# The in-place scaling of raw weights on GpSimd: a scalar per partition in place of a product with a spread tensor

## The chip, the cores and the metric

The kernel runs on one core of a Trainium2 chip. The metric is the device time in microseconds (us) of one execution of the whole program. Five engines work side by side and meet through semaphores: TensorE (PE in the profile, with its weight loads as PEld), VectorE (DVE), ScalarE (ACT), GpSimd (POOL) and SyncE (SP), which here issues the DMAs. Each engine takes its own instructions strictly in the order in which the program holds them.

## The reference

One pre-norm decoder layer on x, 8 sequences of 128 tokens by 512 features, in three parts, each added to x:

```python
x = x + _L0_attn_ref(_layernorm(x), w_q, w_k, w_v, w_o)      # 32 heads, 8 KV heads, head size 128, causal
x = x + _L0_xattn_ref(ctx, ctx, _layernorm(x))               # one head per sequence, 128 x 128 scores over 512 features
x = x + _L0_ffn_ref(_layernorm(x), gate..., up..., down...)  # 4-bit packed weights, inner size 1376
```

Self-attention, the part around the change, is

```python
q = (h @ w_q).reshape(B, S, 8, 4, 128); k = (h @ w_k).reshape(B, S, 8, 128); v = (h @ w_v).reshape(B, S, 8, 128)
probs = softmax(where(causal, q k^T / sqrt(128), -inf))
out = (probs v).reshape(B, S, 4096) @ w_o
```

w_q is 512 x 4096, w_k and w_v are 512 x 1024, w_o is 4096 x 512, all float32.

## The kernel before

Matrix products are made in pairs of float16: each operand is split in a high part and the rest that the high part leaves out, and a product is the sum of three matmuls (`mm3`, lines 162 to 164: high by high, high by low, low by high). A weight must therefore go through three steps before PE can use it: it is multiplied by a scale that brings it into the range of float16, the high part is a cast to float16, and the low part is the difference.

The work goes by KV heads (`g` = 0 to 7), each in two halves of four sequences, 64 attention steps in all. A step works on one head group and one sequence (`g`, `b`): `att_s` makes the scores of the next step, the softmax (`softmax_rows`, line 558: DVE takes the maxima at L611, ACT the exponentials at L568, DVE the reciprocals at L576, POOL multiplies them by a constant at L578) and the probabilities, which POOL normalises (`s`, L625), ACT casts (`pb`, L116), POOL subtracts (`pb`, L119) and a transposing DMA on SP's queue (L639) turns into `pt`. `att_v` multiplies by v, and its result is split into `ah` (ACT) and `al` (DVE). `att_o` multiplies by w_o and DVE adds into x at L665.

Beside these steps the weights of the next head groups are made ready. `fetch_wq`, `fetch_wk`, `fetch_wv` and `fetch_wo` load raw float32 weights into `rawq`, `rawk`, `rawv` and `rawo` (`rawq`, `rawv`, `rawo` have one buffer each, `rawk` two, so a load must wait until its buffer has been read for the last time). `sumsq` (ACT, L260) sums squares, `scales` (a small matmul and three DVE instructions, the last one the reciprocal at L312) makes a scale per matrix or per head, equal on all partitions, in `scq`, `sck`, `scv`, `sco`. Then `prep_wq`, `prep_wk`, `prep_wv` and `prep_wo` call `convert` on pieces of 128 x 512: the function that the change touches. For the first pieces (`direct`) ACT and DVE do it from the raw weight in two instructions. For all others POOL first scales the raw weight in place (L356), ACT casts (`split`, L116) and POOL subtracts (L119). There are 71 such pieces: 30 of `rawo`, 28 of `rawq`, 7 of `rawk`, 6 of `rawv`. The function `at` hangs these calls on attention steps (lines 1130 to 1150), and `pace["mul"]` keeps a scaling behind the normalisation (L625) of the step that it hangs on.

The order on each engine is not the order of the text. The kernel is built with `schedule_with_timeline_sim=True` (line 1480): a planner takes instructions whose inputs are ready on its own clock, which runs on its own costs, by their place in the text, and the order that comes out is fixed in the program. Orders written out by hand are laid over this: `issue_after` for single instructions, `in_order` for the beginning and, on PE and POOL, for the last attention steps. In the middle, the place of the scalings between the other POOL instructions is the planner's.

After the attention steps come the cross-attention (woven into the last ones) and the feed-forward part (`Chain`, lines 1184 to 1197), in which no raw weight is scaled on POOL. Its weights are unpacked by DVE during the attention steps (`dequant`, L810 and L814), from the loads at L794 and L802 on SP's queue.

Of the kernel before, what the change touches and what calls it, by code (L numbers as in the profile page):

```python
# [14 lines left out]
ALU = mybir.AluOpType  # L15
# [38 lines left out]
def tile_decoder(  # L54
# [19 lines left out]
    nc = tc.nc  # L74
# [40 lines left out]
    def split(hi, lo, src, lo_eng=None):  # L115
        a = nc.scalar.copy(hi, src)  # L116
        if hi.dtype == F32R:
            hi = hi.bitcast(F32)
        b = (lo_eng or nc.vector).tensor_tensor(lo, src, hi, ALU.subtract)  # L119
        return a, b  # L120

    def issue_after(later, earlier):


        tc.add_manual_dep(
            later.ins,
            earlier.ins.name,
            mybir.DependencyInfo(mybir.DependencyClass.NoSync, mybir.DependencyReason.DATA),
            reason="pace",
        )  # L130
# [217 lines left out]
    def convert(hi, lo, raw, sc, direct=False):  # L348
        if direct:
            a = nc.scalar.activation(hi, raw, AF.Copy, scale=sc)  # L350
            b = nc.vector.scalar_tensor_tensor(lo, raw, sc, hi, ALU.mult, ALU.subtract)
            return a, b
        wide = sc
        while len(wide.shape) < len(raw.shape):
            wide = wide.unsqueeze(2)
        a = nc.gpsimd.tensor_tensor(  # L356
            raw, raw, wide.to_broadcast(list(raw.shape)), ALU.mult
        )
        if pace:
            issue_after(a, pace["mul"])  # L360
        b, c = split(hi, lo, raw, nc.gpsimd)
        return a, b, c

    def prep_wq(g, j, direct=False):
        hi = wqp.tile([P, KT, P], F16, name="wqh", tag="wqh")
        lo = wqp.tile([P, KT, P], F16, name="wql", tag="wql")
        wq_t[g * GH + j] = hi, lo
        raw = raw_t["q", g][:, :, j * P : (j + 1) * P]
        return convert(hi, lo, raw, sc_t["q", g][:, j : j + 1], direct)

    def prep_wk(g, direct=False):
        hi = wkp.tile([P, KT, P], F16, name="wkh", tag="wkh")
        lo = wkp.tile([P, KT, P], F16, name="wkl", tag="wkl")
        wk_t[g] = hi, lo
        return convert(hi, lo, raw_t["k", g], sc_t["k", g], direct)

    def prep_wv(pr, i, direct=False):
        hi = wvp.tile([P, 2, 2 * P], F16, name="wvh", tag=f"wvh{i}")
        lo = wvp.tile([P, 2, 2 * P], F16, name="wvl", tag=f"wvl{i}")
        wv_t[pr, i] = hi, lo  # L380
        raw = raw_t["v", pr][:, 2 * i : 2 * i + 2, :]
        return convert(hi, lo, raw, sc_t["v", pr], direct)
# [1102 lines left out]
```

## Time and profile before

| | |
|---|---|
| time, median of 3 runs | 661.36 us (659.74 to 665.2) |
| span of the profiled execution | 659.3 us, 0.4 under the lowest and 2.1 under the median of the runs |
| mean granted TensorE clock | 0.995 |
| PE busy | 630.6 us (96%) |
| DVE, ACT busy | 469.9 us (71%), 440.4 us (67%) |
| POOL busy | 395.8 us (60%), 586 instructions |
| of it the scalings at L356 | 31.4 (`rawo`) + 29.2 (`rawq`) + 7.3 (`rawk`) + 6.2 (`rawv`) = 74.1 us, 71 instructions |
| first and last scaling | 48.4 us and 429.6 us from the start |

The profile is of one execution. No other time is told of that execution than its span, from its first to its last instruction; the runs' times are beside it. Busy time is what an engine worked; a group's row gives its line, engine, operation, tiles, shapes and count, then busy time and mean duration, then the idle time of the engine just before these instructions and what ended it. Matmuls overlap each other: a product of 512 columns is listed with some 378 ns, while the next starts 216 ns after it, so the idle time of PE is a safer reading than its busy time.

### The profile page before, as it was taken

The page shows a single profiled execution, that of the slowest core. Times are in us where ns is not written, and L with a number is a line of the kernel's source. Part 1 is how long each engine was busy: PE and PEld are TensorE (multiplying, and loading weights), DVE is VectorE, ACT ScalarE, POOL GpSimd, SP SyncE. Part 2 cuts the span into 40 slices and gives each one's busy share as a digit, 9 for nine tenths or more (in the row PEclk, how much of TensorE's full clock was granted, in tenths as well). Part 3 has the DMA queues.
Part 4 walks back from the last instruction along what each step waited for, and adds up shares of the span by engine and source line. Part 5 has one row for each costly group of instructions (what it writes and reads, how often), then busy time and mean ns, then how long its engine had stood idle before and what let it go on. Part 6 is the DMA issues. An engine that isn't in the chain of part 4 may idle for free.

```text
span 659.3 us, 12426 instructions
## 1 busy us (share of the span) xinstructions
PE 630.6 (96%) x3992; PEld 341.9 (52%) x3992; DVE 469.9 (71%) x1474; ACT 440.4 (67%) x1238; POOL 395.8 (60%) x586
## 2 busy tenths in 40 slices
PE   8789999899999999999999999899998988999996
PEld 5455545455655555565555565456554444445443
DVE  6845786656767776675778565677776768988986
ACT  5676677465758574666677565976566578867674
POOL 7757497664747795556588597663576247622521
PEclk9999999999999999999999999999999999999998
DMA  9277244945553755455547514242544243112002
GB/s 316 54 174 146 84 46 133 229 105 158 121 157 80 192 130 153 109 152 140 144 112 163 149 37 120 46 103 57 90 76 70 41 86 55 22 27 65 1 1 64
DMA packets 117773, 69.34 MB, mean 105 GB/s; under 512 B 84190, under 2 KB 100593, under 8 KB 117708
## 3 DMA queue, kind: packets, MB, share of 16 engines
q1 hardware_dynamic: 117708, 68.55, 43.7%
q8 instruction: 31, 0.51, 0.3%
q14 instruction: 34, 0.28, 0.1%
HBM read 42.12 MB, written 2.20 MB: 67 GB/s over the span
## 4 chain that ended last, share of the span: by engine, by line
PE 56%; POOL 13%; DMA 10%; DVE 8%; issue 7%; ACT 5%; SPq 1%; DVEq 0%; POOLq 0%; ACTq 0%
PE ps_c L1184 6%; PE ps_c L1185 6%; PE ps_o L164 5%; PE ps_o L162 5%; PE ps_o L163 5%; PE ps_q L163 5%; PE ps_q L162 5%; PE ps_q L164 5%; DMA pt<-pb 3%; DMA rawq<-in_L_attn_w_q_dram 3%; POOL pb L119 3%; DMA rawo<-in_L_attn_w_o_dram 2%; POOL s L625 2%; POOL wql L119 1%; POOL rawo L356 1%
## 5 line engine op out<-in xcount | busy, mean ns | idle before, releaser
L568 ACT ACTIVATE s<-s,negm 128x64 f32<-128x64 f32 (+1 forms) x256 | 93.1, 365 | 31.6 <-DVE negm L611 31.3
L162 PE MATMUL ps_o<-woh,ah 128*128 128x512 f16 x256 | 97.1, 379 | 3.2 <-ACT ah L116 3.2
L162 PE MATMUL ps_q<-hT,wqh 128*128 128x512 f16 (+1 forms) x260 | 98.2, 378 | 1.7 <-DVE ql L119 1.7
L163 PE MATMUL ps_q<-hT,wqh 128*128 128x512 f16 (+1 forms) x260 | 98.2, 378 | 0.0
L164 PE MATMUL ps_q<-hT,wql 128*128 128x512 f16 (+1 forms) x260 | 98.0, 377 | 0.0
L164 PE MATMUL ps_o<-woh,al 128*128 128x512 f16 x256 | 96.9, 379 | 0.6 <-DVE al L119 0.6
L163 PE MATMUL ps_o<-wol,ah 128*128 128x512 f16 x256 | 97.0, 379 | 0.0
L119 POOL TENSOR_TENSOR pb<-s,pb 128x256 f16<-128x256 f32 (+1 forms) x128 | 71.7, 575 | 14.8 <-ACT pb L116 12.4
L665 DVE SCALAR_TENSOR_TENSOR xr<-ps_o,unsc,xr 128x512 f32<-128x512 f32 x64 | 47.8, 747 | 42.5 <-PE ps_o L164 41.9
L611 DVE CUSTOM_DVE_ANT_0 s<-ps_sc,mask,soft 128x64 f32<-128x64 f32 (+1 forms) x256 | 66.9, 309 | 4.3 <-PE ps_sc L164 2.0
L578 POOL TENSOR_SCALAR rec<-rec 128x4 f32<-128x4 f32 x64 | 14.8, 231 | 90.1 <-DVE rec L576 87.4
L625 POOL TENSOR_TENSOR s<-s,rec 128x128 f32<-128x128 f32 (+1 forms) x128 | 64.3, 523 | 4.5
L116 ACT CAST pb<-s 128x256 f16<-128x256 f32 (+1 forms) x128 | 43.0, 350 | 33.7 <-POOL s L625 30.0
L119 DVE TENSOR_TENSOR ql<-ps_q,qh 128x512 f16<-128x512 f32 x64 | 43.9, 686 | 28.8 <-ACT qh L116 28.6
L116 ACT CAST ah<-ps_at 128x512 f16<-128x512 f32 x64 | 37.1, 581 | 23.3 <-PE ps_at L164 10.1
L119 DVE TENSOR_TENSOR al<-ps_at,ah 128x512 f16<-128x512 f32 x64 | 43.7, 683 | 7.0 <-ACT ah L116 6.6
L568 ACT ACTIVATION_READ_ACCUMULATOR s<-s,negm 128x1 f32 x256 | 48.1, 188 | 0.0
L116 ACT CAST qh<-ps_q 128x512 f16<-128x512 f32 x64 | 36.7, 573 | 14.0 <-PE ps_q L164 12.5
L1197 DVE TENSOR_SCALAR ps_c<-ps_c,rTg 128x512 f32<-128x512 f32 (+1 forms) x56 | 40.7, 750 | 7.1 <-PE ps_c L1185 6.8
L356 POOL TENSOR_TENSOR rawo<-rawo,sco 128x512 f32<-128x512 f32 x30 | 31.4, 1053 | 22.5 <-DVE sco L312 20.3
L1195 ACT ACTIVATE ps_c<-ps_c,rTu 128x512 f32<-128x512 f32 (+1 forms) x57 | 36.3, 659 | 11.3 <-PE ps_c L1185 9.2
L164 PE MATMUL ps_sc<-k,ql 128*128 128x64 f16 (+1 forms) x256 | 42.7, 206 | 0.5 <-DVE ql L119 0.5
(243 smaller groups left out, 1728.9 us busy)
## 6 DMA issues: line engine op xcount, KB each, us to landing
rawq<-in_L_attn_w_q_dram SPq DMA_DIRECT2D x8, 1024.0 KB
rawo<-in_L_attn_w_o_dram SPq DMA_DIRECT2D x8, 1024.0 KB, 6.0
zi<-zd SPq DMA_DIRECT2D x26, 256.0 KB, 4.1
vd<-v SPq DMA_DIRECT2D x64, 64.0 KB, 2.6
qr<-_L_ffn_down_qweight_dram SPq DMA_DIRECT2D x10, 256.0 KB
xr<-in_x_dram SPq DMA_DIRECT2D x8, 256.0 KB, 7.7
rawk<-in_L_attn_w_k_dram SPq DMA_DIRECT2D x8, 256.0 KB, 4.5
rawv<-in_L_attn_w_v_dram SPq DMA_DIRECT2D x4, 512.0 KB
```

Source lines behind the costliest of these rows:

```text
L116: a = nc.scalar.copy(hi, src)
L119: b = (lo_eng or nc.vector).tensor_tensor(lo, src, hi, ALU.subtract)
L162: nc.tensor.matmul(ps, lh, rh, start=start and i == 0, stop=False)
L163: nc.tensor.matmul(ps, lh, rl, start=False, stop=False)
L164: nc.tensor.matmul(ps, ll, rh, start=False, stop=stop and i == n - 1)
L568: exp = nc.scalar.activation(v, v, AF.Exp, bias=negm[:, j : j + 1], scale=-1.0, accum_out=sums[:, j : j + 1],)
L611: nc.vector.tensor_tensor_reduce(view, flat(ps, cols[j]), masks[j // 2], soft_t[g][:, j % 2 : j % 2 + 1], BIG, ALU.add, ALU.min, negm,)
L625: mul = nc.gpsimd.tensor_tensor(v, v, rec[:, 2 * k : 2 * k + 2].unsqueeze(2).to_broadcast([P, 2, (k + 1) * HQ]), ALU.mult,)
L665: return nc.vector.scalar_tensor_tensor(xr[b], ps, unsc_t[g], xr[b], ALU.mult, ALU.add)
L1184: nc.tensor.matmul(ps, lh, rh, start=r == 0, stop=False, skip_group_check=r > 0)
L1185: nc.tensor.matmul(ps, lh, rl, start=False, stop=True, skip_group_check=r > 0)
L1197: nc.vector.tensor_scalar(ps, ps, sc, None, ALU.mult)
```

## The change

The scaling of a raw weight stays on POOL, in place, with the same 71 calls and the same order in the text. Before, it was a product of two tensors: the second one is the scale's one column, read again for each element of the row (`to_broadcast`). After, it is `tensor_scalar` with the scale's column as the scalar of each partition, and one tensor input.

```diff
-        wide = sc
-        while len(wide.shape) < len(raw.shape):
-            wide = wide.unsqueeze(2)
-        a = nc.gpsimd.tensor_tensor(
-            raw, raw, wide.to_broadcast(list(raw.shape)), ALU.mult
-        )
+        a = nc.gpsimd.tensor_scalar(raw, raw, sc, None, ALU.mult)
         if pace:
             issue_after(a, pace["mul"])
         b, c = split(hi, lo, raw, nc.gpsimd)
```

## The prediction

> **What bounds the kernel now.** I read the page's table of engines first, then the rows by slice.
>
> ```profile
> PE 630.6 (96%) x3992; PEld 341.9 (52%) x3992; DVE 469.9 (71%) x1474; ACT 440.4 (67%) x1238; POOL 395.8 (60%) x586
> ...
> PE 8789999899999999999999999899998988999996
> ...
> POOL 7757497664747795556588597663576247622521
> ```
>
> PE is busy almost throughout, POOL in six tenths. A faster POOL can therefore pay only where PE stands idle for something that comes through POOL. To see where, I cut the span where the scalings begin and end (48.4 and 429.6 us) and at PE's stalls. The columns are the stretch, its length, then the busy time of PE, PEld, DVE, ACT and POOL, then clock and DMA.
>
> ```profile
> 48.00:80.00 32.00, 32.00 (x188) 17.36 (x186) 20.13 (x71) 21.34 (x57) 19.35 (x23) 0.95 0.54 131
> 80.00:130.00 50.00, 47.33 (x316) 25.36 (x315) 35.15 (x130) 33.45 (x109) 37.96 (x57) 1.00 0.55 123
> 130.00:226.00 96.00, 96.00 (x649) 54.60 (x648) 63.53 (x209) 61.38 (x200) 62.06 (x94) 1.00 0.52 131
> ...
> 270.00:366.00 96.00, 95.49 (x643) 53.02 (x642) 68.16 (x225) 63.29 (x206) 64.85 (x96) 1.00 0.54 134
> ...
> 380.00:404.00 24.00, 23.94 (x171) 14.15 (x169) 14.07 (x53) 15.20 (x48) 23.41 (x32) 1.00 0.18 39
> 404.00:432.00 28.00, 25.08 (x166) 12.92 (x165) 18.13 (x73) 21.86 (x69) 18.45 (x28) 1.00 0.35 96
> ```
>
> From 130 to 226 us PE has no idle time, though POOL spends 62 of 96 us there: what is saved on POOL in such a stretch is worth nothing. PE's idle time is 2.67 us in 80:130, 2.92 in 404:432, and 0.06 + 0.51 + 0.07 + 0.06 in the four stretches between (226:270, 270:366, 366:380, 380:404). That is **6.3 us in all where scalings run**, and nearly the ceiling of the direct gain. One stretch is different: in 380:404 POOL itself is full, 23.41 of 24 us. The list of waits says what PE idles for:
>
> ```profile
> PE ps_at L648 <- DMA pt<-pb: 4.2, 6, 1.7
> ...
> PE ps_o L162 <- ACT ah L116: 3.2, 3, 2.6
> ```
>
> Both come through POOL: `pt` is the transposed `pb`, which POOL finishes at L119. The 2.6 us wait for `ah` is at 413 us, and the chain of waits explains it (start, length, what; all in us):
>
> ```profile
> 400.84 1.00 POOL rawo L356
> 401.84 0.71 POOL rawq L356
> 402.55 0.25 issue
> 402.80 1.05 POOL pb L119 x2
> 403.85 1.12 POOL wol L119
> 404.97 0.12 SPq L639
> ...
> 405.18 6.66 DMA rawo<-in_L_attn_w_o_dram
> 411.84 0.02 issue
> 411.86 0.05 ACT junk L260
> ```
>
> The single `rawo` buffer comes free when POOL has made the last `wol` of the head before, at 404.97. Only then is the next load issued. ACT has the sum of squares of that load at the head of its queue and stands still (2.64 us) until 411.86; the exponentials, and then `ah`, are queued behind it, and PE waits for `ah`.
>
> **The change, step by step.** It removes 71 products and adds 71 operations of another kind, on the same engine and the same data. No DMA, wait or tile is added. The rows that price it:
>
> ```profile
> L356 POOL TENSOR_TENSOR rawo<-rawo,sco 128x512 f32<-128x512 f32 x30 | 31.4, 1053 | 22.5 <-DVE sco L312 20.3 <-ACT junk L260 2.1
> L1002 POOL TENSOR_SCALAR h<-xr,rs,rstd 128x512 f32<-128x512 f32 x16 | 12.3, 767 | 1.2
> L421 POOL TENSOR_SCALAR h<-xr,rs,rstd 128x512 f32<-128x512 f32 x8 | 6.4, 796 | 0.8
> L1229 POOL CAST it<-pr 128x512 f16<-128x512 f32 x7 | 4.3, 610 | 31.4 <-DVE pr L1217 31.3
> ```
>
> The old form's median is 1.039 us. No row shows `tensor_scalar` with one operation and a column as scalar at this size. The nearest is L1002: same engine, shape and type, two columns as scalars, two operations, 0.767 us. Below it lies the cast, with no scalar, at 0.61; above it the slowest two-tensor form of the size that runs in these stretches, `wol` at L119 with 1.179. I take 0.767, as the kind of instruction is the same and a missing second operation should not cost time. So one scaling saves 1.039 - 0.767 = 0.27 us (bounds: a gain of 0.43, a loss of 0.14), and POOL's busy time falls by 71 x 0.27 = **19 us**, from 395.8 to about 376.5 (bounds 30 less, 10 more).
>
> On the path to the end, stall by stall, in the old order:
>
> - 413 us (2.60 us). From 380.5 us to the last `wol`, POOL works through 9 scalings with hardly a pause. All move the release of `rawo` forward: 9 x 0.27 = 2.4 us at most. What may become late instead is the reciprocal (DVE, L576) that POOL's L578 needs: it ended at 389.86 and 397.57, while POOL came to it at 392.22 and 398.58, so 2.4 and 1.0 us of slack. By the second, 7 scalings have saved 1.9; of these 1.0 is safe, the rest only as far as the exponentials move up too, and they partly do, because ACT's casts of `pb` before them wait for POOL (1.69 and 3.03 us). Between 1.0 and 2.4 I take **1.8**.
> - 122 us (1.75 us, for `pt`). The chain runs back over the `zi` load (issued at 113.69, behind a transposing DMA that waited for POOL on SP's queue) to two scalings at 108.68 and 109.68: **0.54**.
> - 88 us (0.93 us, for `pt`). One scaling on the chain, at 80.03, then a `wol` and `pb`: **0.27**.
> - 272 us (0.51 us, for `pt`). One scaling at 267.52 between `s` and `pb`: **0.27**. ACT's second cast of `pb` ends some 1.4 us after the start of `s` (at 399.88 and 401.29 in a step of the same form), and a short scaling would end at 0.96 + 0.75 = 1.7, so the cast doesn't become the next wait.
>
> Sum: 1.8 + 0.54 + 0.27 + 0.27 = 2.9 us. All else of the 19 us lies beside a full PE. After 430 us nothing is scaled; the later parts start earlier and keep their length. The span becomes 659.3 - 2.9 = 656.4, and with the 2.1 us by which the median of the runs lies above the span, **658.5**.
>
> [...]
>
> **The planner is the unknown.** The order on POOL is its own: at 394.45 and 395.44 two scalings stand between `s` and `pb` of one step, though in the text they follow `pb`. If the planner charges the new form otherwise than the old one, it may order POOL, ACT, PE and SP otherwise in all of 48 to 430 us. Nothing in the trace shows its costs. This can gain or lose; the rivals price it.
>
> **The rivals.**
>
> 1. *Hidden anyway* (about 661.4). The saved time goes into idle time in front of L578 (POOL waited 73.6 us for L576 between 48 and 435 us). For it: most of POOL's stretches. Against it: 380:404, where POOL is full.
> 2. *Not what it says* (661 to 663). The form takes as long as the old one, or up to 1.18. At 0.14 more each, the same chains (13 scalings) lose 1.8 us.
> 3. *All stalls go* (653 to 655). Shorter scalings, or an order that uses them, remove all 6.3 us: 655.1; and a quarter of PE's 5.9 us of idle time in 480:550 besides: 653.6. Against it: the `zi` load takes 4.4 us and the transposes 2.8 to 6.0 whatever POOL does.
> 4. *Slower by a new order* (about 670). The mechanism is the one seen at 405 to 415: a sum of squares on ACT, or a scaling on POOL, placed ahead of a softmax while its input is not there yet. POOL stood idle 20.3 us in 4 places for `sco` and 15.7 in 5 for `scq`, so the planner's clock runs ahead of the chip already; of these, only one led to a stall of PE of over 2 us. A new order that turns three more of these nine waits into stalls like that at 413 us (2.60 idle and 0.16 in the pipeline, 2.8 each) costs 8.3: 669.7. It decides once a wait is longer than the lead that the softmax has over PE, and the steps at 88, 122 and 272 show that this lead is at times nothing.
>
> **How the numbers follow.** One per cent is 6.6 us, about what a measurement of this kernel can tell from no change. Forecast (656 to 661) 0.48, hidden 0.12, not what it says 0.05, all stalls gone 0.14, slower by order 0.21. Of the last, 0.02 stays under 668 (one or two new stalls, 664 to 667); of "all stalls gone", 0.01 stays above 654.7. So faster by over 1% 0.13, within 1% 0.68, slower 0.19. The range reaches from 653, under the case in which all stalls go, to 670, where three new stalls end; about 0.15 is left out, most of it above.
>
> **What would show it.** L356 as TENSOR_SCALAR x71 at 0.75 to 0.80 us, 54 us in all; POOL near 376 us. PE's wait for `ah` near 413 us under 1.6 us, with ACT's wait for `rawo` as much shorter; the waits for `pt` near 88, 122 and 272 shorter by 0.3 to 0.5. PE still full in 130:226. Wrong would be: other neighbours of the scalings on POOL, or new waits of PE for `ah` or `pt` where there were none, which is rival 4; a mean near 1.04, which is rival 2; POOL down by 19 us and PE's idle time as before, which is rival 1.

## The result, and the profile after

The changed kernel takes **670.54 us** (median; 669.02 to 675.36) where the kernel before, run beside it, takes 660.82: a ratio of **1.0152** with an interval of 1.011 to 1.0195. It is slower by 1.5%; the forecast was 658.5.

The page of the changed kernel, its table of engines and two rows by slice (line numbers behind line 353 are five lower than before: L356 is now L353, L568 L563, L639 L634):

```profile
span 667.4 us, 12412 instructions
...
PE 634.4 (95%) x3992; PEld 342.4 (51%) x3992; DVE 473.7 (71%) x1474; ACT 436.6 (65%) x1238; POOL 433.6 (65%) x586
...
PE   8799999999999989999998989999998988999996
...
POOL 7759698764849789558596989582567247622521
```

POOL did not lose 19 us of work but gained 37.8 (395.8 to 433.6). The groups on POOL by form (busy time, mean ns of one, then the engine's idle time before them) say why:

```profile
L353 POOL TENSOR_SCALAR rawo<-rawo,sco 128x512 f32<-128x512 f32 x30 | 47.4, 1589 | 15.1 <-DVE sco L312 12.5 <-ACT junk L260 2.2 <-DVE scx L312 0.4
L353 POOL TENSOR_SCALAR rawq<-rawq,scq 128x512 f32<-128x512 f32 x28 | 44.1, 1580 | 16.2 <-DVE scq L312 12.7 <-DVE sck L312 3.5
L997 POOL TENSOR_SCALAR h<-xr,rs,rstd 128x512 f32<-128x512 f32 x16 | 12.3, 767 | 1.2
```

The new form takes 1.58 us where the product of two tensors took 1.04, and twice what the other `tensor_scalar` on the same shape takes in the same trace (L997, 0.767). Seventy-one of them take 112.0 us instead of 74.1.

PE's stalls, cut as in the prediction (the stretch, its length, then the busy time of PE, PEld, DVE, ACT and POOL, then clock and DMA):

```profile
80.00:130.00 50.00, 47.80 (x299) 24.87 (x298) 37.16 (x130) 32.05 (x101) 42.74 (x54) 1.00 0.47 106
130.00:226.00 96.00, 96.00 (x655) 54.79 (x654) 64.05 (x210) 60.05 (x200) 66.89 (x89) 1.00 0.50 128
226.00:270.00 44.00, 40.87 (x264) 21.82 (x263) 30.70 (x106) 30.60 (x105) 37.28 (x49) 0.96 0.75 174
270.00:366.00 96.00, 94.84 (x627) 52.61 (x625) 62.06 (x206) 57.04 (x186) 63.98 (x85) 1.00 0.50 130
366.00:380.00 14.00, 12.39 (x93) 6.45 (x91) 11.59 (x35) 7.99 (x27) 14.00 (x19) 1.00 0.29 61
380.00:404.00 24.00, 21.74 (x141) 12.79 (x140) 12.34 (x47) 15.41 (x48) 20.50 (x25) 1.00 0.56 117
404.00:432.00 28.00, 28.00 (x179) 14.31 (x177) 17.11 (x66) 19.44 (x64) 19.87 (x31) 1.00 0.28 74
```

PE is still full from 130 to 226 us. The stall at 413 us is gone (28.00 of 28), but 226:270 now loses 3.13 us where it lost 0.06, 366:380 1.61 (0.07) and 380:404 2.26 (0.06). From 80 to 432 us that is 10.4 us of idle PE against 6.3. The last scaling starts at 436.7 us instead of 429.6: 7.1 of the 8.1 us by which the span grew are lost by then. Idle time is only a part of them: in 226:270 the clock was 0.96 as well, and 0.04 of 44 us is another 1.8 us by estimate. PE's waits name the links:

```profile
PE ps_o L162 <- ACT ah L116: 5.6, 5, 2.6
...
PE ps_at L643 <- DMA pt<-pb: 2.3, 5, 1.0
PE ps_o L164 <- DVE al L119: 1.8, 4, 0.8
```

The wait for `pt` has fallen from 4.2 to 2.3 us and the wait for `ah` has risen from 3.2 to 5.6. So the stalls are not simply the old ones made longer. The chain of waits at the longest of them (start, length, what):

```profile
227.37 0.10 POOL pb L119
227.47 6.79 DMA rawo<-in_L_attn_w_o_dram
234.28 1.15 ACT junk L260 x2
235.44 0.48 ACT ah L116
```

ACT waited 3.83 us at the head of its queue for a load of `rawo` still on its way, then made the sum of squares, and only then the `ah` that PE stood still for. It is the mechanism that the prediction read at 405 to 415 us of the kernel before, in a place where it was not before. And the order did change: going by operation and tile names in the two traces, 171 of POOL's 586 places and 549 of the 1230 on ACT that name a tile now hold another instruction. Two things have changed at once, then: the price of a scaling, and the order on the engines.

### The profile page after: what moved, and what is told of

Same layout as the page of the kernel before. It is cut to its first block, busy times and chain, and to the rows that moved or that the text cites. A ratio compares the mean times of both kernels' runs of the same rounds, so it can differ in the third digit from the quotient of the medians.

```text
span 667.4 us, 12412 instructions
## 1 busy us (share of the span) xinstructions
PE 634.4 (95%) x3992; PEld 342.4 (51%) x3992; DVE 473.7 (71%) x1474; ACT 436.6 (65%) x1238; POOL 433.6 (65%) x586
## 4 chain that ended last, share of the span: by engine, by line
PE 59%; DVE 11%; POOL 9%; ACT 9%; DMA 8%; issue 4%; SPq 0%; DVEq 0%; ACTq 0%; POOLq 0%
PE ps_c L1179 6%; PE ps_c L1180 6%; PE ps_o L164 5%; PE ps_o L162 5%; PE ps_o L163 5%; PE ps_q L162 5%; PE ps_q L164 5%; PE ps_q L163 5%; DMA rawq<-in_L_attn_w_q_dram 3%; ACT s L563 2%; POOL rawq L353 2%; POOL pb L119 2%; PE ps_v L162 2%; PE ps_v L164 2%; PE ps_v L163 2%
## 5 line engine op out<-in xcount | busy, mean ns | idle before, releaser
L563 ACT ACTIVATE s<-s,negm 128x64 f32<-128x64 f32 (+1 forms) x256 | 93.0, 364 | 47.3 <-DVE negm L606 47.0
L353 POOL TENSOR_SCALAR rawo<-rawo,sco 128x512 f32<-128x512 f32 x30 | 47.4, 1589 | 15.1 <-DVE sco L312 12.5
L353 POOL TENSOR_SCALAR rawq<-rawq,scq 128x512 f32<-128x512 f32 x28 | 44.1, 1580 | 16.2 <-DVE scq L312 12.7
L563 ACT ACTIVATION_READ_ACCUMULATOR s<-s,negm 128x1 f32 x256 | 48.0, 188 | 0.0
```

The source lines that it names most:

```text
L353: a = nc.gpsimd.tensor_scalar(raw, raw, sc, None, ALU.mult)
L563: exp = nc.scalar.activation(v, v, AF.Exp, bias=negm[:, j : j + 1], scale=-1.0, accum_out=sums[:, j : j + 1],)
```

## The experiments

### What the form itself costs

Thirteen forms, six times each, alone on POOL, chained so that they run one after the other (eight of them here; the comments give the lines of the profile):

```diff
+    many(lambda: g.tensor_tensor(a, a, spread, ALU.mult))               # L88
+    many(lambda: g.tensor_scalar(a, a, one, None, ALU.mult))            # L89, the new form
+    many(lambda: g.tensor_scalar(a, a, one, 1.0, ALU.mult, ALU.mult))   # L90
+    many(lambda: g.tensor_scalar(a, a, 1.0, None, ALU.mult))            # L91
     ...
+    many(lambda: g.tensor_scalar(a, a, one, one, ALU.mult, ALU.mult))   # L93
+    many(lambda: g.tensor_scalar(a, a, nil, None, ALU.add))             # L94
     ...
+    many(lambda: g.tensor_scalar(half, half, one, None, ALU.mult))      # L97, 256 columns
     ...
+    many(lambda: g.tensor_scalar(half, half, one, 1.0, ALU.mult, ALU.mult))  # L99
```

> Nothing of the decoder is computed: POOL alone runs 13 forms on float32 tiles of 128 partitions, six times each, one after the other; x is copied to the output. The profile after shows the new scaling with a mean of 1.58 us, where 0.767 was taken from the form with two operations. Theory A: the form with a single operation is what is slow; then all forms with one operation at 512 columns (column or constant, multiply or add, in place or not) take 1.55 to 1.60 and those with two 0.75 to 0.80. Theory B: what is slow is a multiplication as the first operation (the fast row subtracts first); then multiply and multiply take 1.5 to 1.6 too, and a single addition 0.75 to 0.80. Theory C: writing in place; then the form with another destination takes 0.75 to 0.80. The product of two tensors takes 1.04 in each. If the cost is per element, 256 columns take about 0.8 and 1024 about 3.1 in the slow form.

The groups on POOL by form in this kernel (busy time, mean ns of one):

```profile
L89 POOL TENSOR_SCALAR big<-big,one 128x512 f32<-128x512 f32 x6 | 9.4, 1563 | 0.6
...
L94 POOL TENSOR_SCALAR big<-big,nil 128x512 f32<-128x512 f32 x6 | 9.4, 1562 | 0.6
L91 POOL TENSOR_SCALAR big<-big 128x512 f32<-128x512 f32 x6 | 8.9, 1488 | 0.5
L88 POOL TENSOR_TENSOR big<-big,one 128x512 f32<-128x512 f32 x6 | 6.2, 1038 | 3.5 <-DMA big<-in_x_dram 3.1
L97 POOL TENSOR_SCALAR big<-big,one 128x256 f32<-128x256 f32 x6 | 5.5, 922 | 0.6
L93 POOL TENSOR_SCALAR big<-big,one 128x512 f32<-128x512 f32 x6 | 4.6, 767 | 0.6
...
L90 POOL TENSOR_SCALAR big<-big,one 128x512 f32<-128x512 f32 x6 | 4.2, 692 | 0.6
...
L99 POOL TENSOR_SCALAR big<-big,one 128x256 f32<-128x256 f32 x6 | 2.9, 478 | 0.6
```

On 512 columns every form with **one** operation takes 1.49 to 1.56 us, whether it multiplies or adds, by a column or by a constant, in place or (1.563) to another tile, flat or (1.562) on a strided view. Every form with **two** takes 0.69 to 0.77. A second operation that multiplies by 1.0 makes the instruction 2.26 times as fast. From 256 to 512 columns one operation adds 641 ns (2.5 ns per column), two add 214 (0.84); some 0.28 and 0.26 us do not depend on the size. So the slow part is paid per element. Theory A of the expectation holds, B and C do not. What inside POOL makes it so, no run here shows.

### Price and order apart

With `planned` and `pin` a kernel is built with one form in the order that the planner made for another. The order is planned once, kept by place in the text, and each instruction is chained to the one before it on its engine, without a wait (shortened):

```diff
+    order = planned(new_nc, "tensor_tensor")   # or "one": each engine's order, by place in the text
     ...
         tile_decoder(tc, *args)
+        for places in order.values():
+            for a, b in zip(places, places[1:]):
+                tc.add_manual_dep(made[b], made[a].name, NoSync)
```

The new form in the old order, and the old form in the new one:

> The new operation, with every engine held to the order that the planner made for the kernel before (each engine's instructions are chained). Theory P (price): the operation is 0.55 us longer at 71 places, and the old order has little room for it where POOL is full; 9 of them lie ahead of the load of rawo at 405 us alone, so 5 us there, and half to one us each at 88, 122 and 272 us: 668 to 674 us, at least as slow as the kernel after. Theory O (order): the longer operation hides in idle time of POOL and the loss of the kernel after is its new order: 661 to 664 us.

> The old product of two tensors, with every engine held to the order that the planner made for the kernel after. Theory P: at the old price the new order is about as good as the old one: 659 to 663 us. Theory O: the order carries the loss: 668 to 671 us.

The chaining itself was controlled with the old form in its own order:

> A control: the old product, every engine held to its own old order by the same chaining as in the other runs. If chaining does nothing but fix the order, the time is that of the kernel before, 659 to 662 us; anything else is a cost of the chaining and has to be taken off the runs in the old order.

| time in us, ratio to before [95%] | old order | order of the changed kernel |
|---|---|---|
| product of two tensors, 1.04 us | 661.3, 1.001 [0.9992, 1.0028] | 667.4, 1.0105 [1.0064, 1.0145] |
| one operation, 1.58 us | 679.2, 1.0279 [1.0251, 1.0307] | 670.5, 1.0152 [1.011, 1.0195] |

In the traces of all four kernels each engine's operations and tiles stand in the order that the table says. The chaining, controlled in the old order, costs nothing that can be measured. In the old order the price alone costs some 18 us, more than either theory had put it (668 to 674 at most). The new order alone costs 6 to 7 us at the old price, between the two theories. Together they cost less than the price alone: **the planner's new order gives back about 8.7 us of what the form costs**, and is itself worse than the old order as long as a scaling is cheap.

PE's waits with the new form in the old order show the price at work (waited for, us in all, times, longest):

```profile
PE ps_at L648 <- DMA pt<-pb: 15.8, 16, 4.5
PE ps_o L162 <- ACT ah L116: 5.0, 6, 1.8
```

Four windows of the same kernel, with the columns as above:

```profile
80.00:130.00 50.00, 44.15 (x270) 22.53 (x269) 30.28 (x116) 30.69 (x99) 42.64 (x54) 0.97 0.50 108
...
122.00:126.00 4.00, 0.20 (x2) 0.18 (x2) 2.54 (x4) 1.09 (x3) 4.00 (x6) 1.00 1.06 174
126.00:130.00 4.00, 4.00 (x14) 1.56 (x13) 0.75 (x2) 0.71 (x2) 1.71 (x2) 0.58 0.72 133
404.00:432.00 28.00, 23.61 (x151) 12.52 (x150) 12.48 (x48) 15.66 (x50) 22.28 (x30) 1.00 0.33 84
```

PE now waits sixteen times for `pt`, 15.8 us in all, where it waited six times for 4.2: `pt` comes through POOL, and in the old order scalings stand between `s` and `pb`. The stall at 122 us grows to 4.5 us while POOL works through (4.00 of 4), and behind it the clock falls to 0.58 for the last window before 130 us. So these are stalls of the old kind, for `pt`, longer and more of them.

The old form in the new order has other stalls. Its list of PE's waits:

```profile
PE ps_o L162 <- ACT ah L116: 5.5, 3, 2.8
...
PE ps_o L164 <- DVE al L119: 2.5, 4, 1.6
PE ps_at L648 <- DMA pt<-pb: 1.8, 3, 1.0
```

And two of its windows:

```profile
226.00:270.00 44.00, 40.62 (x271) 22.06 (x270) 30.26 (x97) 29.44 (x99) 36.34 (x52) 1.00 0.77 169
...
380.00:404.00 24.00, 21.05 (x131) 12.11 (x129) 12.47 (x38) 13.38 (x38) 17.97 (x23) 0.93 0.36 88
```

They stand where those of the changed kernel stand, and are about as large (3.38 and 2.95 us against 3.13 and 2.26), though each scaling takes 0.54 us less. So the waits for `ah` at these two places come with the order, the many waits for `pt` in the old order with the price.

### The fast forms of the same instruction

If the single operation is the whole fault of the form, a second operation that changes nothing should give what the prediction wanted. Built with the planner's own order, and held to the old order and to that of the changed kernel (what the edits here and below come to; in the runs the form is chosen in a helper):

```diff
-        a = nc.gpsimd.tensor_scalar(raw, raw, sc, None, ALU.mult)
+        a = nc.gpsimd.tensor_scalar(raw, raw, sc, 1.0, ALU.mult, ALU.mult)
```

> A scalar per partition as in the kernel after, but with a second operation, a multiplication by 1.0; the planner makes its own order. Theory A: each scaling takes 0.75 to 0.80 us, POOL's busy time is near 376 us, and the forecast's sum can be seen at last: 656 to 661 us, or up to 666 where the new order costs something. Theory B: each takes 1.5 to 1.6 and the time is that of the kernel after, 668 to 672 us.

> The scaling with two operations (0.692 us in the run that measured the forms, 0.347 less than the old product) in the old order, so that nothing but the price changes. The forecast's own sum with this price: 0.347 x 9 ahead of the load of rawo at 405 us, capped by the wait of 2.6 us there, take 2.2; 0.69 at 122, 0.35 at 88, 0.35 at 272 us; 3.6 in all, 657 us. The rival (hidden anyway): POOL's saved time goes into waits for other engines, 660 to 661 us.

> The short scaling with two operations in the order that the planner made for the kernel after. With the old product this order took 667 us, 7 more than the old order. If that loss hangs on the places of the sums of squares and loads in the order (ACT waiting for a load at 231 and 385 us) and not on POOL's speed, the time stays at 664 to 667 us; if POOL's speed sets it, it falls by the same 3 us as in the old order or more, to 660 to 664.

And once with the multiplication as the second operation, behind an addition of zero, in the old order:

```diff
+        a = nc.gpsimd.tensor_scalar(raw, raw, 0.0, sc, ALU.add, ALU.mult)
```

> The scaling as the addition of 0.0 and a multiplication by the scale, the two-operation form that the forecast took its price from (0.767 us), in the old order. The forecast's sum as it stands: 2.9 us less than before, 657.5 us; slower than the run with 0.692 by under 1 us. The rival (hidden anyway): 660 to 661 us.

| time in us, ratio to before [95%] | order |
|---|---|
| 654.5, 0.9904 [0.9889, 0.992] | two multiplications, old order |
| 654.2, 0.9898 [0.988, 0.9915] | addition and multiplication, old order |
| 661.9, 1.0022 [1.0008, 1.0036] | two multiplications, the planner's own, a third order |
| 669.5, 1.0138 [1.0116, 1.0159] | two multiplications, order of the changed kernel |

**The two forms with two operations, held to the old order, beat the kernel before by about 1.0%, and the changed one by more.** Both are faster than the 657 and 657.5 us that were expected, and a scaling takes 0.69 us in the second too, not 0.767. A group on POOL of the first:

```profile
L1447 POOL TENSOR_SCALAR rawo<-rawo,sco 128x512 f32<-128x512 f32 x30 | 20.6, 690 | 22.5 <-DVE sco L312 20.3 <-ACT junk L260 2.2
```

Five windows of the same kernel:

```profile
48.00:80.00 32.00, 30.85 (x192) 17.21 (x192) 20.34 (x75) 22.69 (x63) 16.58 (x24) 1.00 0.55 135
80.00:130.00 50.00, 48.49 (x323) 26.01 (x322) 35.61 (x132) 34.26 (x112) 35.49 (x58) 1.00 0.55 129
...
270.00:366.00 96.00, 96.00 (x643) 52.94 (x641) 68.22 (x229) 64.56 (x214) 61.69 (x99) 1.00 0.52 132
...
380.00:404.00 24.00, 24.00 (x174) 14.34 (x173) 14.14 (x55) 15.79 (x48) 20.77 (x30) 1.00 0.34 81
404.00:432.00 28.00, 28.00 (x188) 14.96 (x187) 19.83 (x88) 22.45 (x73) 19.43 (x32) 1.00 0.37 89
```

A scaling takes 0.690 us, POOL falls to 372.5 us, and the stalls at 413 and 272 us are gone; from 80 to 432 us PE idles 1.51 us instead of 6.29, against 1.15 more in 48:80. That is 3.6 of the 5.8 us by which the two profiled spans differ. By estimate 1.6 of the rest is the clock: it was 0.95 in 48:80 of the kernel before and 1.00 here. The old form held to the new order had such a stretch too, elsewhere (0.96 in its first 48 us, 1.00 in 48:80); that the form removes it is not shown.

Read across, the price matters much in the old order: 0.69, 1.04 and 1.58 us give 654.5, 661 and 679. In the order of the changed kernel no difference shows: 669.5, 667.4 and 670.5, with intervals that overlap. The run with the short form there was expected at 660 to 667. Its stalls are those of the other two prices, 3.49 and 2.87 us in the same two windows:

```profile
PE ps_o L162 <- ACT ah L116: 5.8, 3, 2.8
```

```profile
226.00:270.00 44.00, 40.51 (x271) 22.02 (x269) 29.20 (x99) 29.35 (x101) 33.72 (x52) 1.00 0.73 169
...
380.00:404.00 24.00, 21.13 (x139) 12.47 (x138) 11.19 (x38) 13.38 (x38) 17.23 (x25) 1.00 0.46 94
```

And the same cheap instruction costs 654.5, 661.9 or 669.5 us by the order around it; in the order that the planner makes for it, the good form gains nothing.

### Where the new order loses

The chain at 234 us suggests one cause: on ACT a sum of squares stands ahead of a cast to `ah`. In the old form held to the new order ACT waits for the load of such a sum at 232, 260, 356 and 384 us (3.96, 1.25, 1.81 and 2.3 us). First, in both forms, the cast was moved ahead of the sum of squares at three of these places, 232, 260 and 384 us (shortened, as is the next edit):

```diff
+    for k in (36, 39, 54):          # of ACT's sums of squares, in the order of the changed kernel
+        n = act.index(sums[k])
+        act.insert(n, act.pop(next(m for m in range(n, len(act)) if act[m] in highs)))   # the next ah
```

> The old product in the new order, with one thing changed in the order of ACT: at three places (near 232, 260 and 385 us) the cast of ah stands before the sum of squares of a load that is still on its way, and no longer behind it. If these three places carry the loss of the new order, PE's waits for ah there (1.3, 1.4 and 2.8 us, and the half clock that followed the last one) go, and the time falls from 667 to 660 to 663 us. If the loss is spread over the order, it falls by under 2 us, to 665 or more.

> The kernel after (the scaling with one operation, in its own order), with the same three casts of ah moved ahead. If the same places carry the loss, the waits of 2.6, 0.3 and 2.1 us and the half clock after the first go: from 670.5 to 663 to 666 us, though each scaling still takes 1.56 us. If the longer scaling is what holds the kernel after up, the wait comes back elsewhere and the time stays at 668 to 671.

It gave 666.9 us (1.0095 [1.0062, 1.0128]) with the old form and 672.6 (1.0185 [1.0158, 1.0213]) with the new one: no gain. A line of PE's waits in the first of the two:

```profile
PE ps_o L164 <- DVE al L119: 6.9, 6, 3.2
```

The waits for `ah` are gone from the head of the list, and PE waits for `al` instead (6.9 us where it was 2.5). In the stall of 3.2 us that begins at 384 us DVE makes that `al` only after a reciprocal that itself waits for ACT's exponentials, and these are still behind the sum of squares. Freeing one of the two consumers of the same late load freed nobody here.

Second, the loads of the sums at 232, 356 and 384 us, where ACT waited longest, were moved ahead on SP's queue. They had been issued some 3 to 4 us after their buffer was free (224.28 after 220.33 us, 349.38 after 346.0, 377.94 after 374.7), behind other entries of the queue:

```diff
+    for k, ahead in [(36, 3), (51, 2), (54, 4)]:   # the load of that sum of squares, entries moved ahead
+        n = sp.index(load_of[k])
+        sp.insert(n - ahead, sp.pop(n))
```

> The old product in the new order, with three loads moved ahead on SP's queue: rawo near 224 us ahead of three other entries, rawo near 349 us ahead of two, rawq near 378 us ahead of four. In that order each stood 3 to 4 us after its buffer was free (220.3, 346.0 and 374.7 us), behind transposes and loads that waited for other engines, and ACT stood still 4.0, 1.8 and 2.3 us at the sums of squares of these loads. If the late loads carry the loss of the new order, ACT's waits and the waits of PE behind them go (1.3 to 1.5, 1.6 to 1.8 and 2.8 us, and the half clock after the last): from 667 to 660 to 663 us. If not, 665 or more.

> The kernel after (one operation, its own order) with the same three loads moved ahead on SP's queue. The buffers come free later here, since POOL takes 1.56 us for each scaling, so less is to be had than with the old product: from 670.5 to 664 to 668 us if the late loads carry a part of the loss. If the longer scaling alone holds it up, 669 to 672.

Also no gain: 666.6 us (1.0087 [1.0061, 1.0113]) and 672.2 (1.0169 [1.0113, 1.0225]). With the old form the stall at 232 us disappeared, but from 48 to 440 us ACT then waited 11.0 us, five times, for the transpose that frees `pb` (5.5, four times, without the move). The longest of these waits is for a transpose that one load had overtaken: issued at 376.36 us (376.68 without the move), it took 6.08 us to land, and ACT went on at 382.52 instead of 380.69. Near 385 us PE still waited for `ah`. The two rows, ACT's and PE's:

```profile
ACT pb L116 <- DMA pt<-pb: 11.0, 5, 4.2
...
PE ps_o L162 <- ACT ah L116: 4.6, 2, 2.6
```

Third, one engine alone was held to the order of the changed kernel, with the old form, and the planner ordered the others around it:

```diff
-        for places in order.values():
+        for places in [order[e] for e in HELD]:    # PE, or POOL, or ACT
```

> The old product; PE alone is held to the order of the kernel after, the planner orders the other engines around it. If PE's order (which matmuls stand before which attention step) carries the 7 us that the new order costs at the old price, 666 to 669 us. If the order of another engine does, 659 to 663.

> The old product; POOL alone is held to the order of the kernel after. If the place of the scalings between the softmax steps on POOL carries the loss, 666 to 669 us; if not, 659 to 663.

> The old product; ACT alone is held to the order of the kernel after. If the place of the sums of squares and casts on ACT carries the loss, 666 to 669 us; if not, 659 to 663. If all three of these runs come out slower by 3 us or more, the loss belongs to no engine: then most orders other than the old one are slower, and the old one is a good draw.

They gave 684.6 us (1.0366 [1.0351, 1.0382]) for PE, 669.1 (1.015 [1.0111, 1.0189]) for POOL and 679.6 (1.0286 [1.0262, 1.031]) for ACT. All three are slower than the whole new order or like it, so the loss was not traced to one engine; POOL's came out about where a theory had put it (666 to 669), the other two far above both. It is a weak test, as the other engines then have an order that is neither the old nor the new one.

**What is settled and what is open.** That the new order costs 6 to 15 us against the old one, at equal price, is shown at two prices, 6 to 7 us at 1.04 and 15 at 0.69. Which edge of the order costs it is not: two repairs of a visible stall only moved the wait, and the tests of single engines singled out none. At the prices 0.69 and 1.04 every order other than the old one was slower; at 1.58 the new one is faster. That speaks for the old order being an unusually good one, among those that the planner can give, as long as scalings are short; but this is argued, not shown.

## Why the prediction failed, by its steps

- **The bound held.** With all engines held to the old or the new order, PE is full in 130:226 at every price but for one operation in the old order, which loses 1.53 us there. What is lost or won shows in PE's stalls, and in the clock behind some of them (0.50 in the changed kernel, 0.58 with one operation in the old order).
- **The price is the step that failed.** "I take 0.767, as the kind of instruction is the same and a missing second operation should not cost time." It costs 0.8 to 0.9 us: the form takes 1.56 alone and 1.58 in the kernel, outside the bounds of 0.61 to 1.18, so POOL's work grew by 37.8 us where the sum took 19 away. The nearest row differed in just the property that decides, and it was set aside by an argument that no row carried. The bound above was taken from the slowest two-tensor form, as if a form with less to do could not be slower.
- **The sum of the stalls was too small, even for a fast form.** It gave 2.9 us for 0.27 us per scaling, and 3.6 for 0.35 when it was redone before the run. At 0.35, in the old order, the runs gave 6.4 and 6.7. The term for 413 us was put at 1.8 of 2.60 (2.2 when redone), and the stall went whole; that at 272 us went whole too, where 0.27 of 0.51 was taken. From 80 to 432 us that is 4.8 us less of idle time; a part of the rest is the clock, which the sum did not hold. "All stalls go" (653 to 655) has the time of a fast form in the old order, though 1.51 us of stalls are left there.
- **The same chains counted too little on the other side.** "Not what it says" named the right kind of case, with 13 scalings on the path: at 0.54 us more each that would be 7.0 us. The price alone costs 18. When scalings get longer, more of them come onto the path: PE's waits for `pt` went from 6 to 16.
- **"Slower by a new order" had the right mechanism.** Its place, a sum of squares on ACT ahead of a softmax while the load is on its way, is what the chain at 234 us shows, and its 669.7 is near 670.5. But that the number agrees is in part luck: its sum holds three new stalls and no dearer scaling, and the order alone, at the old price, gives 667.4. The order accounts for 6 to 7 us at the old price; in the changed kernel it softens a price that alone gives 679.
- **What would show it** read right: L353 at 1.58 instead of 0.75 to 0.80 and POOL at 433.6 instead of 376 refute the price, the new waits for `ah` show the order.

## What to carry to other kernels

Price an instruction by a row that has the same number of operations and the same kinds of operands, or measure it alone; that a form with less to do is no slower is a guess, and here it was wrong by a factor of two. On POOL a `tensor_scalar` on float32 rows of 256 or 512 should be given a second operation, if only a multiplication by 1.0: here that took 0.48 us instead of 0.92 on 256 columns, and 0.69 instead of 1.56 on 512. Where a planner orders the program, compare two forms in a held order before saying what the form is worth: at the price 0.69 two orders that the planner chose itself, each for another form of this kernel, lie 15 us apart, more than twice what the good form gained.

## What the hardware showed that was not expected

- POOL's `tensor_scalar` on 128x512 float32 takes 1.56 us with one operation (1.49 with a constant), 0.69 with a column and a constant, 0.77 with two columns; a product of two tensors takes 1.04.
- After a stall of 2.6 us PE was granted half the clock (0.50) for about 3 us. Three windows of the changed kernel, around this stall, which ends at 235.96 us:

```profile
234.00:237.00 3.00, 1.04 (x4) 0.45 (x5) 1.06 (x5) 2.71 (x6) 0.18 (x1) 0.94 1.46 179
237.00:240.00 3.00, 3.00 (x11) 1.22 (x10) 2.40 (x14) 2.47 (x12) 3.00 (x3) 0.50 0.64 145
240.00:244.00 4.00, 4.00 (x41) 2.79 (x40) 3.15 (x7) 3.10 (x7) 4.00 (x4) 1.00 0.00 0
```

The granted clock is 0.50 in the second window, and matmuls of 512 columns start 0.42 us apart there instead of 0.216; PE counts as fully busy all the while. At half pace these 3 us hold 1.5 us of work less, so by this estimate the stall costs some 4 us and not 2.6. Yet the stalls at 413 us in the kernel before (2.6 us) and in the old form held to its own order (3.1 us) were followed by a clock of 1.00. So the half clock came after one stall of 2.6 us and stayed away after another, and after one of 3.1. What tells them apart was not settled.
